# Due times of the output projections in an attention and feed-forward block

## The chip, the core and the metric

The kernel runs on one core of a Trainium2 chip. The time is the device time of one execution in microseconds (us), and the figure quoted is the median of several executions. Five engines run side by side, each through its own instructions in a fixed order: TensorE (PE in the profile; its weight loads are listed as PEld), VectorE (DVE), ScalarE (ACT), GpSimd (POOL) and SyncE (SP), which here only issues transfers. An instruction waits until what it depends on is done, and everything behind it on its engine waits too.

## The reference

The input is x of 4 batches, 1024 rows and 512 columns, in 32-bit floats. There are two halves, each wrapped in layer norms and added back to its input:

```python
x = x + layernorm(attn(layernorm(x)))
x = x + layernorm(ffn(layernorm(x)))

def attn(x):                       # 16 heads of 32
    q, k, v = split(x @ Wqkv + bqkv)
    scores = einsum("bsnh,btnh->bnst", k, q) / sqrt(32)
    scores = triu(scores) + -10000.0 * tril(ones, k=-1)
    attn = softmax(scores, axis=2)
    out = einsum("bnkq,bknh->bqnh", attn, v)
    return out @ Wo + bo
```

The feed-forward half multiplies by gate and up weights of 2048 x 512 and a down weight of 512 x 2048, held as small integers with a zero point and scales. The change touches the attention half only.

## The kernel before

**Periods.** The four batches are worked off one after another. In each, four groups of four heads (the index `hb`, also called a head block here) follow each other. A head block takes 12 *periods*: 4 for the first 512 rows of the softmax axis (`g` is 0) and 8 for the second (`g` is 1). So there are 48 periods a batch and 192 in all, numbered `p` from 0; 12 more (-12 to -1) lead in. In this text the *phase* of a period is `p` modulo 12. In one period the program issues, in this order:

- `weights` for one tile of 128 keys, in two halves `u` of two heads each: PE puts minus the maximum (L359) and the scores (L367) into PSUM, ACT takes the exponential (L384), and in the periods on the diagonal (phases 0 to 3 and 8 to 11) POOL cuts off the triangle (L386);
- `maxima` for a tile that is 12 periods ahead: PE scores (L278), on the diagonal a bound on DVE (L286), and the reduction on DVE (L290);
- `values` of the period before: exponentials times v (PE L406), added up in `po`;
- `add_up`: the exponentials of the tiles are summed for the softmax denominator, by an accumulating transfer issued from POOL (L434) off the diagonal and by POOL additions (L436) on it;
- at the end of phases 3 and 11, `shift_parts`: a chain of small DVE instructions (L300 to L306) that turns the maxima into what the next tiles' exponentials subtract.

Pieces of other work are put in between, by a small planner.

**The planner.** Work with a cost and a due period stands in three queues called lanes: `qk` and `v` (a piece is one projection of 128 columns by 256 rows for four heads, 64 matmuls at L250 in 16 groups of 4, evacuated by ACT at L532 or L535) and `out` (a piece is `project_out(b, j, half)`). Each piece costs `FULL`, 1.75. Every period a budget `spare` grows by `rate(p)`, which is the steepest slope of cost to be done over time left; `fill` takes the lane whose first piece is due earliest as long as the budget allows, or when the piece is already due. A lane is first in, first out. `fill(p, 1)` can put one piece in the middle of a period (after the `weights`, `maxima` and `values` of `u` 0), and `fill(p, 9)` puts the rest at its end. In what follows a piece in the middle is marked @0 and a piece at the end @2. Apart from these, at most one of the `whole` pieces goes into a period: a stage of the layer norm (`ln_stage`; from the fourth on it has four PE transposes, L515), the transposes of v (`turn_piece`, L544), the scan of v on DVE (`later_v`, L552), the transposes of the maxima (`shift_rows`, L314) and the part of the masked keys (`masked_part`, L326). A `turn_piece` can go only once the v pieces it needs are out, and a scan only once its turns are.

**An output projection.** `project_out(b, j, half)` computes half the columns of 128 rows of batch b. Its instructions: for half 0 a load of the input rows `xo` on SP (256 KB, L560); on PE 64 matmuls at L250 into `py`; on DVE the bias addition that empties `py` into `y` (L567); and for half 1 the following. First `store_out(b, j - 1)` for the rows before: DVE normalizes `y` (L86), POOL adds `y` to `xo` (L579), SP stores `xo` (L580, 256 KB). Then the statistics of its own `y`: DVE L76 and L77, POOL L79 and L80. `y` and `xo` have two buffers each, so the first L567 of rows j + 1 needs the L579 of rows j - 1 done. `y`'s PSUM tile comes from `projected`: the first piece of a half period uses a bank of its own (`ps_own`), and any further one the two buffers of `ps_big`, which it shares with the `maxima` tiles, with the second `weights` tile of some periods and with the transposes.

**Where they stand.** `after` is the first period of the next batch, `at[b, 0, 0] + 48`. The pieces of batch b may start at `after - 3` (rows 0 to 511, j under 4) or `after + 5` (j from 4 on). All 16 are due at `after + 39`:

```python
due = after + 39
put(lanes["out"], FULL, min(due, n_periods - 1 if j < 4 else n_periods + 9),
    lambda p, t=after - 4 + WAIT if j < 4 else after + 4 + WAIT: p >= t,
    project_out, b, j, half)
```

In the order that comes out, the pieces of batch 0 stand in periods 59 (one), 70 and 71 (three) and 78 to 85 (twelve); those of batch 1 in 107, 118, 119 and 126 to 133; those of batch 2 in 171 to 183, one or two in each; those of batch 3 in 189 to 191 and after the last period. Below, a piece is written OUT b j half: OUT 0 4 1 is `project_out(0, 4, 1)`.

## Time and profile before

| | |
|---|---|
| median of 3 runs | 1933.15 us (1932.91 to 1935.1) |
| time of the profiled execution | 1933.34 us |
| its span, first to last instruction | 1931.6 us |
| mean granted TensorE clock | 0.989 |
| periods 0 to 191 begin at | 79.2 to 1186.2 us |
| DVE busy, whole span | 1223.6 us (63%) |
| ACT busy | 643.1 us (33%) |
| POOL busy | 715.4 us (37%) |
| DVE busy from 344.6 to 635.1 us (batch 1) | 222.4 of 290.5 us |
| POOL busy in the same stretch | 162.2 of 290.5 us |

A period is found in the trace by L359: 768 matmuls, four in each period, so the start of every fourth one begins a period. In the lines of the profile, a group of instructions is named by line, engine and operation, and `out<-in` gives the program's names; in a timeline the first two numbers are start and duration in us, and a bracket gives how long the engine had been idle and what released it.

### The profile page before, as it was taken

The numbers are of one execution on the slowest core, as the hardware profiler recorded it, in microseconds if no ns is written. First come the engines' busy times: TensorE is split into PE (matmuls) and PEld (weight loads), VectorE is DVE, ScalarE is ACT, GpSimd is POOL, SyncE is SP. The second block draws the span as 40 slices with busy tenths as digits, with TensorE's granted clock in tenths as the row PEclk, the third lists the DMA queues.
The fourth block names the chain that finished last, engine by engine and source line by source line (L and its number), as shares of the span: only waits on it lengthen the run. The fifth ranks groups of instructions, "written<-read, shape, count | busy, mean of one in ns | idle before, by whom it ended". The sixth has DMA issues, their size and how long they took to land.

```text
span 1931.6 us, 40959 instructions
## 1 busy us (share of the span) xinstructions
PE 1851.4 (96%) x17761; PEld 1095.2 (57%) x17761; DVE 1223.6 (63%) x1913; ACT 643.1 (33%) x962; POOL 715.4 (37%) x1016
## 2 busy tenths in 40 slices
PE   7899999999989999989999989999999999999997
PEld 3334444444444444444344434788888888888886
DVE  4788888887777777777777875544344444444344
ACT  2244444434424444424444322222222222222221
POOL 2155545554655564655455474102010110101011
PEclk9899999999999999999999999999999999999999
DMA  3254355345245145245134452511010100101000
GB/s 110 66 127 104 79 127 121 79 115 99 49 112 115 25 87 100 59 102 100 23 67 89 116 135 71 190 66 44 1 44 4 41 12 33 40 5 44 1 22 24
DMA packets 65628, 137.48 MB, mean 71 GB/s; under 512 B 6304, under 2 KB 20640, under 8 KB 65440
## 3 DMA queue, kind: packets, MB, share of 16 engines
q0 software_dynamic: 17280, 62.92, 17.6%
q1 hardware_dynamic: 41008, 67.40, 10.5%
q10 hardware_dynamic: 7152, 4.46, 0.8%
q8 instruction: 141, 2.31, 0.5%
q14 instruction: 47, 0.39, 0.1%
HBM read 55.07 MB, written 16.78 MB: 37 GB/s over the span
## 4 chain that ended last, share of the span: by engine, by line
PE 83%; DVE 7%; POOL 5%; ACT 2%; issue 2%; DMA 2%; POOLq 0%; SPq 0%; DVEq 0%
PE pq L250 17%; PE pg L973 12%; PE pu L973 12%; PE acc L1006 12%; PE sc L278 9%; PE po L406 6%; PE st L359 4%; PE st L367 3%; PE py L250 2%; PE pd L417 2%; DVE nm L290 2%; POOL pT L436 1%; ACT pT L384 1%; DMA pT<-pT 1%; POOL xo L579 1%
## 5 line engine op out<-in xcount | busy, mean ns | idle before, releaser
L384 ACT ACTIVATE pT<-st 128x1024 f32<-128x1024 f32 (+3 forms) x384 | 310.2, 811 | 367.7 <-PE st L367 286.8
L290 DVE TENSOR_REDUCE nm<-sc 128x2 f32<-128x1024 f32 (+3 forms) x384 | 366.7, 956 | 102.4 <-PE st L367 82.6
L250 PE MATMUL pq<-xnT,w 128*32 128x256 f32 x6144 | 377.8, 391 | 3.5 <-ACT xnT L516 2.7
L278 PE MATMUL sc<-in,in 32*128 32x512 f32 (+3 forms) x1536 | 346.5, 537 | 16.4 <-DVE nm L290 13.3
L367 PE MATMUL st<-in,in 32*128 32x512 f32 (+3 forms) x1536 | 306.2, 487 | 0.0
L250 PEld LDWEIGHTS pq<-xnT,w 128*32 128x32 f32 x6144 | 186.5, 112 | 204.7 <-issue 83.8
L983 DVE SCALAR_TENSOR_TENSOR h<-pu,pre_us,s 128x512 f32<-128x512 f32 x128 | 96.1, 751 | 311.0 <-PE pu L973 310.2
L1006 PE MATMUL acc<-d,h 128*128 128x512 f32 x896 | 224.8, 393 | 0.2 <-DVE h L993 0.2
L386 POOL TENSOR_SCALAR_AFFINE_SELECT pT<-pT 128x256 f32<-128x256 f32 x256 | 131.8, 538 | 248.9 <-ACT pT L384 248.8
L981 ACT ACTIVATE s<-pg,pre_gs 128x512 f32<-128x512 f32 x128 | 88.1, 688 | 297.7 <-PE pg L973 297.7
L1006 PEld LDWEIGHTS acc<-d,h 128*128 128x128 f32 x896 | 166.0, 188 | 34.2 <-DVE h L993 0.5
L436 POOL TENSOR_TENSOR pT<-pT,pT 128x768 f32<-128x768 f32 (+1 forms) x120 | 183.5, 1550 | 1.8 <-DMA pT<-pT 1.8
L286 DVE TENSOR_TENSOR sc<-sc,bound 128x256 f32<-128x256 f32 x256 | 109.1, 426 | 118.2 <-PE sc L278 76.4
L406 PE MATMUL po<-pT,vt 128*32 128x512 f32 (+3 forms) x1536 | 170.6, 496 | 12.0 <-POOL pT L386 9.6
L79 POOL TENSOR_SCALAR rs_y<-mv_y 128x1 f32<-128x1 f32 x32 | 8.7, 271 | 448.1 <-DVE mv_y L77 448.1
L434 POOL DMA_DIRECT2D pT<-pT x120 | 106.5, 916 | 152.2 <-PE pm L314 57.4
L992 ACT CAST h<-h 128x512 fp32r<-128x512 f32 x128 | 79.4, 621 | 248.4 <-DVE h L983 248.4
L993 DVE TENSOR_TENSOR h<-h,h 128x512 fp32r<-128x512 f32 x128 | 88.7, 693 | 87.9 <-ACT h L992 87.9
L359 PE MATMUL st<-mT,ones_bf 3*128 3x512 bf16 (+3 forms) x768 | 125.4, 331 | 13.8 <-ACT pT L384 13.8
L278 PEld LDWEIGHTS sc<-in,in 32*128 32x128 f32 x1536 | 114.5, 185 | 35.8 <-issue 12.4
L367 PEld LDWEIGHTS st<-in,in 32*128 32x128 f32 x1536 | 134.0, 190 | 0.7
L250 PE MATMUL py<-wo_sb,o 128*32 128x256 f32 x2048 | 121.5, 384 | 7.1 <-DVE y L567 5.1
(136 smaller groups left out, 2572.2 us busy)
## 6 DMA issues: line engine op xcount, KB each, us to landing
pT<-pT POOLq DMA_DIRECT2D x120, 512.0 KB, 5.7
xr<-in_x SPq DMA_DIRECT2D x32, 256.0 KB, 2.8
xo<-in_x SPq DMA_DIRECT2D x32, 256.0 KB, 2.9
x<-xo SPq DMA_DIRECT2D x32, 256.0 KB, 2.0
out<-y SPq DMA_DIRECT2D x32, 256.0 KB, 2.0
look<-in_gate_wt SPq DMA_DIRECT2D x16, 256.0 KB, 3.1
look<-in_up_wt SPq DMA_DIRECT2D x16, 256.0 KB, 2.7
look<-in_down_wt SPq DMA_DIRECT2D x16, 256.0 KB, 3.0
```

Of the source, the lines that this page charges most:

```text
L250: nc.tensor.matmul(out[k * D : (k + 1) * D, :], lhsT=lhsT[:, k * D : (k + 1) * D], rhs=rhs, start=(c == 0), stop=(c == len(pairs) - 1),)
L278: nc.tensor.matmul(sc[:, h % 2, :n], lhsT=qT[h * D : (h + 1) * D, ts(j, P)], rhs=kT[h * D : (h + 1) * D, 512 * k : 512 * k + n], start=Tru ...
L286: nc.vector.tensor_tensor(sc[:, :, n - P : n], sc[:, :, n - P : n], bound.unsqueeze(1).to_broadcast((P, 2, P)), ALU.min,)
L290: nc.vector.tensor_reduce(nm[:, k, jj, 2 * u : 2 * u + 2], sc[:, :, :n], AX.X, ALU.max, negate=True)
L359: nc.tensor.matmul(st[h // 2][:, h % 2, :n], lhsT=ones_bf[h * D : h * D + 3, :], rhs=mT[h * D : h * D + 3, 512 - n :], start=True, stop=False,
L367: nc.tensor.matmul(st[h // 2][:, h % 2, :n], lhsT=kT[h * D : (h + 1) * D, ts(c, P)], rhs=qT[h * D : (h + 1) * D, q0 : q0 + n], start=False ...
L384: nc.scalar.activation(pT[:, :, :n], st[u][:, :, :n], AF.Exp)
L386: nc.gpsimd.affine_select(out=pT[:, :, :P], in_=pT[:, :, :P], compare_op=ALU.is_ge, fill=0.0, base=0, pattern=[[0, 2], [1, P]], channel_mu ...
L406: nc.tensor.matmul(state["po"][h * D : (h + 1) * D, 512 - n :], lhsT=v[:, c, h * D : (h + 1) * D], rhs=pT[:, h, :n], start=(c == 0), stop= ...
L436: nc.gpsimd.tensor_tensor(total[:, :, 512 - n :], total[:, :, 512 - n :], pT[:, :, :n], ALU.add)
L973: nc.tensor.matmul(dst, lhsT=w[i * P // IB][:, c, ts(i % (IB // P), P)], rhs=part[:, c, :], start=(c == 0 and k == 0), stop=(c == HC - 1 a ...
L1006: nc.tensor.matmul(acc[t0][t], lhsT=part[:, ts(t, P)], rhs=dw[i * P // IB][:, i % (IB // P), :], start=(i == 0 and k == 0), stop=(i == IC ...
```

## The change

One line: the pieces of a batch are no longer all due at `after + 39` but one every second period, from `after + 7` to `after + 37`.

```diff
             for j in range(NJ):
                 for half in range(2):
-                    due = after + 39
+                    due = after + 7 + 4 * j + 2 * half
                     put(lanes["out"], FULL, min(due, n_periods - 1 if j < 4 else n_periods + 9),
                         lambda p, t=after - 4 + WAIT if j < 4 else after + 4 + WAIT: p >= t,
                         project_out, b, j, half)
             put(lanes["out"], 0.1, due + 1,
                 lambda p, b=b: state.get(("rows at", b, NJ - 1), p) < p, store_out, b, NJ - 1)
```

Nothing else is edited. The number of instructions on each engine stays as it was; the planner puts them in another order from period 50 on. For the last batch the due times are cut to 191 and 201 as before. The pieces of batch 0 now stand in periods 50 to 84, of batch 1 in 97 to 132, of batch 2 in 146 to 178, and the pieces of q, k and v, the stages of the layer norm and the turns of v move to other periods in between. Periods 176 and 179 to 184 hold none of these pieces any more, where before 176 to 183 held ten output projections.

## The prediction

> **What bounds the kernel now.** The page comes first: PE is busy nearly all the time and fills the chain that ended last. Then the waits of PE and DVE in the attention part, from 344 to 1186 us.

> ```profile
> span 1931.6 us, 40959 instructions
> ...
> PE 1851.4 (96%) x17761; PEld 1095.2 (57%) x17761; DVE 1223.6 (63%) x1913; ACT 643.1 (33%) x962; POOL 715.4 (37%) x1016
> ...
> PE 83%; DVE 7%; POOL 5%; ACT 2%; issue 2%; DMA 2%; POOLq 0%; SPq 0%; DVEq 0%
> ```

> ```profile
> PE py L250 <- DVE y L567: 4.8, 4, 1.4
> PE sc L278 <- DVE nm L290: 3.9, 4, 1.9
> PE sc L278 <- DVE y L567: 3.1, 2, 1.5
> PE pv L544 <- DVE y L567: 2.6, 2, 1.4
> ```

> The reader sees that moving PE work as such gains nothing, and that part of PE's few waits (4.8 + 3.1 + 2.6 = 10.5 us) comes from DVE's emptying of `py`.

> Next I cut the trace into periods by the starts of L359. Their lengths repeat to a hundredth: phase 7 with one piece and one transposing piece takes 5.81 us twelve times, with a second piece 7.53 to 7.54; phase 8 takes 5.47, with transposes 6.18. So a length is a floor of its phase, plus 1.73 a piece, plus 0.66 to 0.7 for transposes, plus a *stall*. The counts of pieces and transposes don't change; only stalls do. Over periods 48 to 179 I add up 41.8 us of them. A quiet phase 0 beside one in the burst of output projections (us from the start, length, busy times, clock):

> ```profile
> core 0: us, PE busy (x) PEld busy (x) DVE busy (x) ACT busy (x) POOL busy (x), PEclk, DMA share, GB/s
> 562.58:572.19 9.61, 6.88 (x97) 3.14 (x94) 8.72 (x20) 2.05 (x2) 5.40 (x8) 1.00 0.15 56
> 635.12:640.54 5.42, 4.88 (x66) 2.16 (x64) 5.14 (x10) 2.05 (x2) 4.59 (x7) 1.00 0.01 3
> ...
> 441.40:445.10 3.70, 3.70 (x34) 1.39 (x34) 2.83 (x5) 0.00 (x0) 1.42 (x3) 0.54 0.24 44
> ```

> The first has one piece more (1.73) and still 2.46 us too many, with DVE at 8.72 of 9.61: on the diagonal DVE is the second bound. The last row is a stretch in which the clock was halved; I come back to it. What stalls in the burst (timeline):

> ```profile
> 553.04 3.79 POOL L436 TENSOR_TENSOR pT<-pT,pT 128x768 f32<-128x768 f32 x2
> ...
> 554.23 0.93 DVE L86 TENSOR_SCALAR y<-y,mv_o 128x512 f32<-128x512 f32 x1
> ...
> 556.80 1.26 POOL L579 TENSOR_TENSOR xo<-xo,y 128x512 f32<-128x512 f32 x1
> ...
> 558.09 0.42 DVE L567 TENSOR_TENSOR y<-py,bo_sb 128x256 f32<-128x256 f32 x1 [2.12 <-POOL xo L579]
> 558.57 0.30 PEld L278 LDWEIGHTS sc<-in,in 32*128 32x128 f32 x4 [1.73 <-DVE y L567]
> ```

> `y` has two buffers. The piece OUT j 1 normalizes and stores rows j - 1; the piece OUT j+1 0 needs that buffer. POOL adds `xo` only after two denominator sums; DVE waits 2.12 us at L567, its maxima behind it wait, and PE's scores behind those. I call OUT j 1 and OUT j+1 0 in one period a *pair*. The last view is the small chain on DVE after phases 3 and 11:

> ```profile
> 945.47 2.50 POOL L436 TENSOR_TENSOR pT<-pT,pT 128x512 f32<-128x512 f32 x2
> 945.60 1.19 DVE L304 TENSOR_TENSOR nm<-nm,wide 128x16 f32<-128x16 f32 x1
> 946.82 1.21 DVE L305 CAST wide<-nm 128x16 bf16<-128x16 f32 x1
> ...
> 949.62 0.30 PEld L278 LDWEIGHTS sc<-in,in 32*128 32x128 f32 x4 [2.70 <-DVE nm L290]
> ```

> Beside POOL's sums these take 1.2 us each; at 564.49 and 564.71, without them, 0.18 and 0.20. PE's scores wait.

> [...]

> **The change, part by part** (positions from the order of instructions of both kernels and the planner's loop).

> *Taken away.* The bursts in periods 80 to 85 and 128 to 132 had stalls of 6.94 and 6.96 us. The turn in period 148 (4.65, the last view) moves to 151, phase 7, where turns stalled 0.00. Periods 172 to 174 had 2.05 with output pieces of batch 2 in them. Sum -20.6.

> *The tail.* Periods 180 to 184 took 25.5 us with five pieces; less 5 x 1.73 that is 16.9. They lose all five. Their floors add up to 16.15; without the maxima (four score matmuls of about 1 us together, four periods) and with three transposes, some 14. So up to -2.9; no wait takes over as long as ACT (2.05 in a phase 0) is under PE. If the cover of the pieces was hiding an exponential's delay, 0. I take -2.0.

> *Turns pushed to the head block's end.* The q, k and v pieces go later, so the turns of the third batch's and second batch's last head block land in phases 11 and 0 (83 and 84, 131 and 132), the scan in phase 2 and the masked part in phase 3 (87, 135). Periods 35 to 41 have just this order, and stall 4.64 us. Twice: +9.3. If the second pieces beside them cover it, 0.

> *Pairs in phases 0 and 4, in the middle and at the end of the period.* Periods 72, 76, 120 and 124. Nearest row: period 84 (OUT 0 6 1 and OUT 0 7 0), 2.46, with 0.51 in the next. Bound below: period 119, two pieces without this wait in it, 0 and 0.25 in the next; above: 131's 3.70. With 2.97 each: 11.9, less the 2.46 that these four places stall today (72: 0.84; 76: 0.67; 120 and 121: 1.47; 124: -0.52): +9.4.

> *Pairs at the end of phase 8.* Periods 80, 128 and 164. Nearest: the pairs at the end of phase 9 (81, 129), after which 82 and 130 stalled 1.38 and 1.20: +1.3 each, +3.9. Bounds 0 and 2.06 (period 83).

> *A turn in period 100, phase 4,* behind a short phase 3. Turns and transposes in phase 4 stalled -0.1 (52), 0.67 (76), 2.96 (112) and 4.65 (148). Where no long phase 3 goes before it is 3 or more: +3.0.

> *Single half-1 pieces where DVE is tight.* In 63, 111, 155, 159 and 167 a piece brings DVE 0.42 (L567) + 0.59 (L86) + 0.69 (L76) + 0.18 (L77) = 1.88 us. All of it on the path would be 9.4, none 0 (phase 7's pieces, 79 and 127, stalled 0.00); half: +4.7.

> *At nothing.* ACT is idle 3.5 us at a time, so its moved evacuations wait on PE alone. On SP each `xo` load stands behind the store of the rows two before, and the loads of the layer norm and of the weight check queue behind it; they are due a period (4 to 9 us) later and land in 2.8 to 3.1, so a late one would first show as DVE waiting at L76 or L589, up to 3 us. On POOL, L579, L79 and L80 (1.3 + 0.3 + 0.6) go ahead of L434's transfers in phases 5 to 9; three `pT` buffers cover that.

> Sum: -20.6 - 2.0 + 9.3 + 9.4 + 3.9 + 3.0 + 4.7 = +7.7 us, on a span of 1931.6. The profiled execution took 1933.34, the median is 1933.15, so the times differ by nothing that matters: 1940.9.

> *The clock.* In periods 64, 112, 131 and 148 the granted clock was halved for 3.4 us, each time after PE's weight loads had paused 1.73 to 2.70 us; 32 matmuls at L250 took 3.56 instead of 1.93, so it costs 1.7. Some sixteen pauses over 1.5 us gave four of these. Seven new pauses would give 1.7 x 7 / 4 = 3.0, but two of the four lie in what is taken away and are in its sum; I leave the new ones to the range.

> [...]

> **The rivals.**

> - *Faster.* The wait for `y` needs POOL to be behind with two sums. In phases 0 and 4 the piece in the middle of a period stands ahead of that period's sums, so L579 may come at once. With 0.25 a pair, and none in phase 8: 7.7 - 4 x 2.72 - 3.9 = -7.1, 1926. It decides once a pair costs under 2.97 - 7.7 / 4 = 1.05 us. Against it: in period 84, the same place, L567 still waited for DVE's own chain.
> - *No change.* One kind of stall for another, as the 13.9 and 12.1 us of stalls in batches 1 and 2 suggest, however their pieces lie: 1933, give or take 3.
> - *Slower still.* Every one of the seven pairs' pauses halves the clock: 7 x 1.7 = 11.9 more, 1952.8. Against it: four in sixteen so far.
> - That it doesn't do what it says is out: the order of instructions shows the pieces spread.

> **How the numbers follow.** Forecast 50 in 100, no change 24, faster 18, slower still 8. The time is the forecast's. A measurement of this kernel tells apart about 0.2%, 3.9 us. Faster by more: 0.19; within: 0.24; slower by more: 0.57. The range leaves out the last case and half of the faster one: 1926 to 1949.

> **What would show it.** In the changed kernel, no DVE wait at L567 in periods 81 to 85; waits at L567 for POOL L579 in 72, 76, 120, 124 and after 80, 128, 164; PE waiting at L326 in 87 and 135; period 100 near 9 us and 148 at 5.4; 180 to 184 at about 15 us together. I am wrong if the pairs pass without a pause, or if other phases' floors move, which would mean that the sum by phases doesn't hold.

## The result, and the profile after

| | before | after |
|---|---|---|
| median | 1934.12 us (4 runs, 1932.91 to 1936.32) | 1959.16 us (4 runs, 1958.22 to 1963.16) |
| ratio | | 1.0132, 95% interval 1.0115 to 1.015 |
| span of the profiled execution | 1931.6 us | 1957.6 us |
| mean granted clock in it | 0.989 | 0.981 |
| half clock within periods 0 to 191 | 17.1 us, 5 windows | 54.6 us, 16 windows |

The kernel became 25 us slower; the forecast was 7.7 us. First the page of the kernel after, the lines that were shown of before:

```profile
span 1957.6 us, 40968 instructions
...
PE 1868.5 (95%) x17761; PEld 1102.3 (56%) x17761; DVE 1222.8 (62%) x1913; ACT 642.8 (33%) x962; POOL 710.3 (36%) x1016
...
PE 83%; DVE 10%; POOL 4%; issue 1%; ACT 1%; DMA 1%; SPq 0%; POOLq 0%; DVEq 0%; ACTq 0%
```

The number of matmuls is the same, yet PE is busy 17 us longer: the same matmuls took longer, as in the windows of half clock, where 32 of L250 take 3.41 us (at 495.25, shown below) instead of the 1.93 of full clock (at 1117.38 of before). DVE's share of the chain rose from 7 to 10%. Then the waits of the attention part, 344 to 1212 us (what waits <- for what: total us, times, longest):

```profile
PEld py L250 <- DVE y L567: 13.8, 5, 3.4
...
PE po L406 <- POOL pT L386: 9.8, 9, 3.1
PE py L250 <- DVE y L567: 9.6, 4, 2.6
...
PE sc L278 <- DVE nm L290: 6.6, 6, 2.5
PEld pd L417 <- DVE y L567: 6.1, 4, 2.6
```

PE's wait of L250 for L567 has doubled (4.8 to 9.6 us), and the row sums of the softmax (`pd`, L417) wait for L567 too. Three stretches of the kernel after: period 72, a pair; period 84, which was in the burst and took 9.61 us; and period 177 in the tail, which took 7.43 us before.

```profile
core 0: us, PE busy (x) PEld busy (x) DVE busy (x) ACT busy (x) POOL busy (x), PEclk, DMA share, GB/s
...
488.38:498.59 10.21, 8.08 (x96) 3.50 (x93) 9.33 (x17) 2.05 (x2) 6.63 (x10) 0.83 0.07 25
568.37:576.69 8.32, 8.32 (x100) 3.97 (x97) 6.97 (x13) 2.52 (x3) 1.87 (x4) 1.00 0.01 2
...
1139.60:1154.11 14.51, 9.65 (x61) 2.77 (x61) 7.53 (x10) 1.62 (x2) 10.59 (x16) 0.65 0.98 217
```

Periods 72 and 177 of the kernel before, for comparison (84 of before was shown with the prediction):

```profile
484.90:491.16 6.26, 4.98 (x64) 2.07 (x60) 5.95 (x15) 2.05 (x2) 5.93 (x9) 1.00 0.46 128
1111.83:1119.25 7.42, 6.19 (x64) 2.28 (x61) 7.05 (x11) 1.62 (x2) 7.34 (x10) 1.00 1.02 242
```

In period 84 PE is now busy throughout: the burst is gone, as forecast. The other two stall, at a granted clock of 0.83 and 0.65. In period 177 POOL is busy 10.59 of 14.51 us.

The period model (floor + 1.73 a piece + transposes + stall) held: in both kernels periods without a stall agree to some 0.05 us. So the 26 us of span can be put down place by place, as the change of the stalls from before to after (windows of half clock that fall there in brackets, before and after). The second profile of after, from the fifth experiment, stands beside it.

| periods | forecast | after | second profile |
|---|---|---|---|
| bursts and turn: 80-85, 128-132, 148, 172-174 | -18.0 (-20.6, and +2.6 for the pairs in 80 and 128) | -17.4 (2; 0) | -17.5 |
| pairs in phases 0 and 4: 72, 76, 120, 124 and the next | +9.4 | +9.7 (0; 3) | +9.5 (3) |
| turns at the block's end: 86-91, 133-139 | +9.3 | +4.3 (0; 1) | +4.3 (1) |
| turn in 100 | +3.0 | +3.2 (0; 1) | +1.6 (0) |
| single pieces: 60-69, 105-119, 145, 155-171 | +4.7, and 1.3 for 164 | +18.7 (2; 4) | +18.5 (4) |
| tail, 175-184 | -2.0 | +9.0 (0; 5) | +9.6 (6) |

The rows of the first profile add up to +27.5 us. All periods together grew by 28.0, and the stretch ahead of period 0, where no output piece stands, was 2.7 us shorter in it (76.49 us instead of 79.15). Four terms came near or stayed below; the single pieces and the tail are what was missed, 13 and 11 us. The timeline of the pair in period 72:

```profile
489.85 1.21 DVE L304 TENSOR_TENSOR nm<-nm,wide 128x16 f32<-128x16 f32 x1
...
490.05 1.90 PE L250 MATMUL py<-wo_sb,o 128*32 128x256 f32 x30
491.09 1.22 DVE L305 CAST wide<-nm 128x16 bf16<-128x16 f32 x1
...
493.04 1.23 DVE L290 TENSOR_REDUCE nm<-sc 128x2 f32<-128x1024 f32 x1
...
494.78 0.41 DVE L567 TENSOR_TENSOR y<-py,bo_sb 128x256 f32<-128x256 f32 x1
...
495.25 3.41 PE L250 MATMUL py<-wo_sb,o 128*32 128x256 f32 x32 [2.13 <-DVE y L567]
```

The first piece is through PE at 491.95, but DVE empties it only at 494.78, behind the small chain and the maxima. The second piece stands first in its half period, so it takes the same bank, `ps_own`, and PE waits. Then it runs at half clock: 32 matmuls take 3.41 us where 30 took 1.90. That isn't the wait of the forecast, which had DVE wait at L567 for a buffer `y` that POOL still read. Between 344 and 1212 us that wait came up 1.1 us in all, in periods 81 and 165. And the tail, period 177:

```profile
1142.61 1.06 POOL L386 TENSOR_SCALAR_AFFINE_SELECT pT<-pT 128x256 f32<-128x256 f32 x1
...
1143.00 3.07 POOL L485 TENSOR_TENSOR o<-t,t 128x128 f32<-128x128 f32 x1
1143.43 2.85 POOL L79 TENSOR_SCALAR rs_f<-mv_f 128x1 f32<-128x1 f32 x1
1143.56 2.28 DVE L552 TENSOR_TENSOR_SCAN vl<-in,zero 128x1024 f32<-128x1024 f32 x1
...
1143.73 1.92 PE L406 MATMUL po<-pT,vt 128*32 128x512 f32 x4 [3.15 <-POOL pT L386]
...
1146.91 0.40 POOL L386 TENSOR_SCALAR_AFFINE_SELECT pT<-pT 128x256 f32<-128x256 f32 x1
```

PE waits for the triangle cut L386, which stands on POOL behind a store's L579, L79 and L80, and again behind an L485 and an L79 that take 3.07 and 2.85 us here, beside a DVE scan of 2.28 (the median of the 124 L485 is 0.46). With no output piece in 176 PE gets there early, its weight loads pause 3.76 and 3.45 us, and it then runs at half clock. In the kernel before, where two pieces stand in 176, the same two waits of PE's matmuls were 0.62 and 0.61 us, against 3.15 and 1.71 here:

```profile
1113.83 1.05 PE L406 MATMUL po<-pT,vt 128*32 128x512 f32 x4 [0.62 <-POOL pT L386]
...
1115.49 1.05 PE L406 MATMUL po<-pT,vt 128*32 128x512 f32 x4 [0.61 <-POOL pT L386]
```

The pieces that the forecast took out of the tail had been work under which POOL caught up.

### The profile page after: what moved, and what is told of

It reads as the page before. It is cut to its first block, busy times and chain, and to the rows that moved or that the text cites. A ratio compares the mean times of both kernels' runs of the same rounds, so it can differ in the third digit from the quotient of the medians.

```text
span 1957.6 us, 40968 instructions
## 1 busy us (share of the span) xinstructions
PE 1868.5 (95%) x17761; PEld 1102.3 (56%) x17761; DVE 1222.8 (62%) x1913; ACT 642.8 (33%) x962; POOL 710.3 (36%) x1016
## 3 DMA queue, kind: packets, MB, share of 16 engines
q0 software_dynamic: 17280, 62.92, 17.4%
## 4 chain that ended last, share of the span: by engine, by line
PE 83%; DVE 10%; POOL 4%; issue 1%; ACT 1%; DMA 1%; SPq 0%; POOLq 0%; DVEq 0%; ACTq 0%
PE pq L250 16%; PE pg L973 12%; PE pu L973 12%; PE acc L1006 12%; PE sc L278 9%; PE po L406 6%; PE py L250 4%; PE st L359 4%; PE st L367 3%; DVE nm L290 2%; PE pd L417 2%; DVE sc L286 1%; POOL pT L436 1%; ACT pT L384 1%; PE pv L544 1%
## 5 line engine op out<-in xcount | busy, mean ns | idle before, releaser
L290 DVE TENSOR_REDUCE nm<-sc 128x2 f32<-128x1024 f32 (+3 forms) x384 | 366.7, 956 | 102.5 <-PE st L367 83.3
L250 PE MATMUL pq<-xnT,w 128*32 128x256 f32 x6144 | 377.1, 390 | 4.0 <-ACT xnT L516 2.7
L278 PE MATMUL sc<-in,in 32*128 32x512 f32 (+3 forms) x1536 | 348.7, 541 | 15.7 <-DVE nm L290 15.7
L250 PEld LDWEIGHTS pq<-xnT,w 128*32 128x32 f32 x6144 | 187.1, 112 | 199.1 <-issue 78.6
L386 POOL TENSOR_SCALAR_AFFINE_SELECT pT<-pT 128x256 f32<-128x256 f32 x256 | 125.9, 508 | 259.4 <-ACT pT L384 259.3
L436 POOL TENSOR_TENSOR pT<-pT,pT 128x768 f32<-128x768 f32 (+1 forms) x120 | 183.5, 1550 | 0.2 <-DMA pT<-pT 0.2
L79 POOL TENSOR_SCALAR rs_y<-mv_y 128x1 f32<-128x1 f32 x32 | 8.7, 270 | 448.2 <-DVE mv_y L77 448.2
L434 POOL DMA_DIRECT2D pT<-pT x120 | 106.4, 925 | 157.0 <-PE pm L314 60.8
L250 PE MATMUL py<-wo_sb,o 128*32 128x256 f32 x2048 | 129.3, 399 | 12.0 <-DVE y L567 9.9
L359 PE MATMUL st<-mT,ones_bf 3*128 3x512 bf16 (+3 forms) x768 | 126.7, 334 | 10.6 <-ACT pT L384 10.0
L278 PEld LDWEIGHTS sc<-in,in 32*128 32x128 f32 x1536 | 115.2, 186 | 36.7 <-issue 15.9
```

Source lines behind the costliest of these rows:

```text
L250: nc.tensor.matmul(out[k * D : (k + 1) * D, :], lhsT=lhsT[:, k * D : (k + 1) * D], rhs=rhs, start=(c == 0), stop=(c == len(pairs) - 1),)
L278: nc.tensor.matmul(sc[:, h % 2, :n], lhsT=qT[h * D : (h + 1) * D, ts(j, P)], rhs=kT[h * D : (h + 1) * D, 512 * k : 512 * k + n], start=Tru ...
L290: nc.vector.tensor_reduce(nm[:, k, jj, 2 * u : 2 * u + 2], sc[:, :, :n], AX.X, ALU.max, negate=True)
L359: nc.tensor.matmul(st[h // 2][:, h % 2, :n], lhsT=ones_bf[h * D : h * D + 3, :], rhs=mT[h * D : h * D + 3, 512 - n :], start=True, stop=False,
L386: nc.gpsimd.affine_select(out=pT[:, :, :P], in_=pT[:, :, :P], compare_op=ALU.is_ge, fill=0.0, base=0, pattern=[[0, 2], [1, P]], channel_mu ...
L436: nc.gpsimd.tensor_tensor(total[:, :, 512 - n :], total[:, :, 512 - n :], pT[:, :, :n], ALU.add)
```

## The experiments

Ratios are against before, run on the same chips, with 95% intervals. Experiments 1 to 4 ran together (before 1935.26 us, 17 runs), 5 to 8 together (1934.03, 8 runs), 9 to 11 together (1936.18, 14 runs). Experiments 5, 6 and 9 are one run each and are read by their profiles. "Stalls" of some periods are their time over the floors of the period model.

### 1. ScalarE empties the output pieces

```diff
-            nc.vector.tensor_tensor(y[:, ts(half, 256)], py, bo_sb[:, ts(half, 256)], ALU.add)
+            nc.scalar.copy(y[:, ts(half, 256)], py)
+            nc.vector.tensor_tensor(
+                y[:, ts(half, 256)], y[:, ts(half, 256)], bo_sb[:, ts(half, 256)], ALU.add
+            )
```

> The changed kernel, but ACT copies each output projection out of PSUM into y (a copy of 128x256, about 0.47 us as the q, k, v pieces take there), and DVE then adds the bias in place in SBUF. Theory 1 (the bank): the projection stays in its one PSUM bank until DVE, busy with the chain L300 to L306, comes to L567, and PE's next piece or the denominator sums L417 wait for that bank. Then the pauses in periods 72, 76, 120, 124, 157, 161 and 169 go, with their half clocks: 1940 to 1946 us, and PE's waits for DVE's L567 (13 us from 344 us on) under 3 us. Theory 2 (the buffer y, the prediction's): y is not free until POOL has added xo; ACT then waits just as DVE did, with the exponentials behind it: 1957 to 1965 us, pauses in the same periods.

Measured: 1962.77 us (1957.06 to 1963.74), 1.0131 [1.0111, 1.0151]: no gain. The four pairs fell from 12.2 to 4.2 us and 157, 161 and 169 from 7.9 to 2.7, as the bank theory has it. But 60 to 69 and 105 to 119 grew by 3.1 and 6.1, and ACT waited for the buffer, PE behind it (waits of this kernel, same stretch). Of the 6.1 us, 4.2 stand in period 105, and 105 grew by 4.2 and 3.7 in experiments 6 and 9 too, where DVE empties as in after: that part can't be put down to the edit.

```profile
ACT y L567 <- POOL xo L582: 16.6, 6, 3.3
...
PEld pd L417 <- ACT y L567: 10.3, 5, 2.6
```

So there are two obstacles in a row: the bank that DVE empties late, and behind it the buffer `y` of the forecast. Freeing the first brings the second to light.

### 2 and 3. Only batches 0 and 1, or only batch 2

```diff
-                    due = after + 7 + 4 * j + 2 * half
+                    due = after + 7 + 4 * j + 2 * half if b < 2 else after + 39
```

(and `b == 2` in the third)

> The new due times for batches 0 and 1 alone; batch 2 is due as before. By the stalls added up period by period, batches 0 and 1 cost 16 us of the 26: 1950 us, give or take 3, with periods 176 to 181 as in the kernel before (8.3 us of stalls). If the loss lies in the emptied tail alone: 1934 to 1938.

> The new due times for batch 2 alone. By the stalls: 10 to 12 us, 1945, give or take 3, of which 9 in periods 176 to 181. If the emptied tail costs nothing and its stalls are those of the layer norm stages, as the prediction had it: 1932 to 1937.

Measured: 1951.36 us (1948.52 to 1955.0), 1.0088 [1.0068, 1.0108], and 1941.25 us (1937.07 to 1944.41), 1.0031 [1.0021, 1.0041]. The first came as expected, the second lay just under its range. The two add up to 1.0119, near the whole change's 1.0132. With batch 2 alone, the tail still went from 5.9 to 13.7 us of stalls, with four windows of half clock: the tail's loss comes from batch 2's pieces leaving it. Its size depends on the profile of before, in which no half clock fell in the tail: in experiments 2, 4 and 8, where the tail's pieces stand as in before, 175 to 184 took 4.3, 4.3 and 2.5 us longer than there, with two, two and one windows. Beside these the tail's loss in after is 5 to 7 us, not 9.

### 4. One piece a period in chosen places

```diff
-                    due = after + 39
+                    due = after + (2, 5, 6, 7, 8, 9, 17, 18, 19, 20, 21, 29, 30, 31, 32, 33)[2 * j + half] if b < 2 else after + 39
+                    t = after - 4 + WAIT if j < 4 else after + 4 + WAIT
...
-                        lambda p, t=after - 4 + WAIT if j < 4 else after + 4 + WAIT: p >= t,
+                        lambda p, t=due if b < 2 else t: p >= t,
...
-                ahead = heads(lanes, p)
+                ahead = heads({k: w for k, w in lanes.items() if k != "out" or most != 1 or p > 144}, p)
```

(against before; the last edit keeps output pieces out of the middle of a period)

> Batches 0 and 1: one piece in each of the periods after + 2, 5 to 9, 17 to 21 and 29 to 33 (phases 5 to 9, and one phase 2), always at the end of the period; batch 2 due as before. Theory 1: in these phases no denominator sum waits for the bank and DVE has no chain, so the bursts' 13.9 us go and only the turns moved to phases 11 and 0 come back (2 to 5 us a batch): 1926, from 1921 to 1931. Rival (spreading costs wherever the pieces stand, because every period then loses cover of another kind): 1940 or more.

Measured: 1940.76 us (1938.46 to 1944.45), 1.0028 [1.0017, 1.0038]: theory 1 missed, the rival's time (1940 or more) came. Bursts (13.9 to 5.5 us) and pairs were gone, but new stalls came in 57 to 59 (6.3 us), 87 (2.3), 105 and 106 (4.3) and 135 (3.8): a second half in phases 7 to 9 puts L579, L79 and L80 (2.1 us on POOL) ahead of the scan and the triangle.

### 5. The kernel after, a second profile

> The kernel after, unchanged, profiled a second time. Theory C (most of what the forecast missed is the granted clock: a pause of PE does or does not bring a window of half clock of about 3.4 us, by where the pause falls on a grid of windows that runs freely): the pauses of PE's weight loads are the same as in the first profile to 0.1 us wherever no half clock lies just before them, but the half clock falls in other periods in part, each window shifts the length of its period by about 1.55 us, and the span differs from 1957.6 us by up to 6 us. Rival (what is slow is fixed by the order of the work): the same periods with the same lengths to 0.1 us, half clock included.

Measured: 1957.82 us, span 1956.1. Periods 36, 100 and 120, first in the first profile of after, then in the second (the columns as above):

```profile
270.53:279.61 9.08, 8.38 (x69) 3.47 (x66) 7.77 (x11) 2.52 (x3) 2.95 (x4) 0.82 0.01 2
...
660.28:669.61 9.33, 8.33 (x69) 3.14 (x66) 7.71 (x11) 2.52 (x3) 6.04 (x9) 0.82 0.00 0
789.34:798.22 8.88, 6.51 (x97) 3.42 (x94) 8.54 (x17) 2.05 (x2) 5.51 (x8) 1.00 0.01 2
```

```profile
272.98:280.52 7.54, 6.84 (x68) 2.93 (x66) 7.25 (x11) 2.52 (x3) 2.95 (x4) 1.00 0.01 2
...
659.23:666.91 7.68, 6.69 (x68) 2.76 (x65) 7.54 (x11) 2.52 (x3) 6.03 (x9) 1.00 0.00 0
788.34:798.44 10.10, 7.76 (x96) 3.38 (x93) 9.30 (x17) 2.05 (x2) 6.37 (x10) 0.83 0.07 26
```

The same instructions, 1.54 and 1.65 us shorter without half clock, and 1.22 longer with it (0.7 net, as the next period gave 0.5 back). The total of half clock after period 48 is the same, 47.8 us, in other places. That agrees with theory C: a pause is where a window of half clock *may* follow, and the program's order alone does not decide whether it does.

### 6 and 9. Filling the pairs' pauses with useless work

> After, with 64 useless matmuls of 1.9 us in all into an unused half of the PSUM bank, just ahead of the second output piece of periods 72, 76, 120 and 124, where PE paused 2.95 to 3.41 us. Theory C: what remains of each pause is 1.0 to 1.5 us, no half clock follows it there, and the four periods are not longer than in after although PE has 1.9 us more to do in each: 8.5 to 8.8 us each. Rival (a pause costs its own length only, the half clock in these periods came from something else): half clock as before in them, and periods longer by up to 1.9 us each. Theory B (the bank is what the second piece waits for): its wait ends at the same time after the first piece as in after, filled or not.

Measured: 2016.32 us. As an experiment on the pauses it failed. A piece is 16 matmul calls (32 in the trace's records, 2048 for 64 pieces), not the 64 that this text gave above; the 64 stood in an order in which none overlaps, took 14 us a time, and waited for L567 like the piece behind them. So once more:

```diff
+            if p in (72, 76, 120, 124):
+                t = ps_big.tile([P, 256], F32, tag="big", name=f"fill_{p}")
+                for c in range(HC):
+                    for k in range(P // D):
+                        nc.tensor.matmul(
+                            t[k * D : (k + 1) * D, :],
+                            lhsT=wo_sb[:, c, k * D : (k + 1) * D],
+                            rhs=wo_sb[:, c, 256:512], start=True, stop=True,
+                        )
             fill(p, 9)
```

> The filler of the sixth experiment was of the wrong size and in the wrong place: 64 matmuls in an order in which they don't overlap, 14.3 us of PE a time, and into the bank under dispute, so that they waited for VectorE too (22.5 us in all). Here after, with the 16 matmuls of one projection piece more (1.73 us by the period model), useless, into another bank, just ahead of the second output piece of periods 72, 76, 120 and 124. Theory C: PE's pauses there shrink from 2.95 to 3.41 us to 1.2 to 1.7 us, and with them the half clock: at most one of the four periods has a window of it, where the two profiles of after have one in or behind three of the four; and no period is longer than its own period in after that had a half clock, though each has 1.73 us more work: 72, 76, 120, 124 and the period behind each cost 10.8 us over their floors and the filler's 6.9 together, against 12.2 and 10.9 in after without any filler. The filler's own time is then covered: the sum over these eight periods is longer than in after by less than 3 us. Rival (the pauses cost their length, the clock is not of their making): longer by 5 to 7 us, half clock as before.

Measured: span 1956.4 us (time 1958.13). Period 72 and 76 with the filler, then 76 without it, in the first profile of after (72 was shown above):

```profile
488.00:497.62 9.62, 8.33 (x128) 4.50 (x125) 9.28 (x17) 2.05 (x2) 6.41 (x10) 1.00 0.02 7
513.45:522.41 8.96, 8.11 (x128) 3.88 (x124) 8.75 (x16) 2.05 (x2) 5.28 (x8) 1.00 0.01 2
```

```profile
514.30:524.21 9.91, 7.35 (x96) 3.20 (x93) 9.19 (x16) 2.05 (x2) 6.15 (x10) 0.90 0.03 10
```

32 matmul records more, and both periods are shorter, at full clock. The eight periods (72, 76, 120, 124 and the next of each) took 63.7 us together, against 66.2 and 66.0 in the two profiles of after, though PE had 6.9 us more to do; half clock there fell from 10.2 us to none. Theory C expected up to 3 us more; they came out 2.4 us less. The whole was not faster than after: half clock fell elsewhere, and 105 and 112 grew by 3.7 and 1.1 us.

### 7. No output pieces in phases 0 and 4

```diff
-                        lambda p, t=after - 4 + WAIT if j < 4 else after + 4 + WAIT: p >= t,
+                        lambda p, b=b, t=after - 4 + WAIT if j < 4 else after + 4 + WAIT: (
+                            p >= t and (b == B - 1 or p % 12 not in (0, 4))
+                        ),
```

> After, with the output pieces of the first three batches barred from phases 0 and 4 of a batch (they go when the next phase opens). Theory B (in these phases the second piece, and the row sums of the softmax behind it, take the one PSUM bank that the first half of the period left full): the pauses of PE in 72, 76, 120, 124, 157, 161 and 169, 12 us together over before in the four pairs and 6 in the three others, go, and little comes in their place, since the pieces go into phases that had none: 1943 us, 1938 to 1948. Rival M (a piece costs the same wait wherever it stands, as in the experiment that gave the emptying to ScalarE): 1955 to 1962 us.

Measured: 1945.18 us (1941.57 to 1949.63), 1.0062 [1.0039, 1.0085], as theory B expected. The pairs' 12.2 us went to -0.6, and 157, 161 and 169 from 7.9 to 1.0; 87 and 135 stalled 5.1 and 3.9 us, with half clock (4.1 and 1.3 in after), and the tail kept its stalls (14.4 in 175 to 184, 14.9 in after). Where a piece stands was worth 14 us of the 25.

### 8 and 11. Two more placements

> One output piece a period, of batches 0 and 1, at the periods 2, 5, 6, 7, 17, 18, 19, 29 to 34, 37, 38 and 39 after the batch's softmax is done, none in phases 0 and 4 and none as a burst; batch 2 as before. It leaves the turns of batch 1 nearly where they were before. Theory B: bursts, bank waits and late turns are all gone, and what is left is half clock at pauses shared with before: 1930 us, 1924 to 1936, below before. Rival M: a piece in the first half of a period delays the POOL or DVE work of that phase by its own 2.1 us wherever it stands, as it did in periods 57 to 59, 87 and 105 of the run with single slots: 1938 to 1946 us.

Measured: 1942.25 us (1938.04 to 1944.3), 1.0043 [1.0028, 1.0058], in the rival's range. The pieces were moved to 2, 5, 6, 7, 17, 18, 19, 29 to 34, 37, 38 and 39 in the diff of experiment 4. PE now waited 3.6 us for the scan in 58 and in 106, each time with half clock behind it.

> Output pieces of batches 0 and 1 at 18, 22, 23, 26, 27, 29, 30, 34, 34, 35, 35, 37, 37, 38, 38 and 39 periods after the batch's softmax is done (batch 2 as before): none in phases 0 and 4, no second half of a tile in phases 7 to 9 where its store on POOL would stand ahead of the scan and the diagonal, and late enough that the q, k and v pieces, the turns and the masked part of the next batch stand where they did in before up to its burst. Theory B: the stalls by the output pieces are then those of pairs in one half period, 0.1 to 0.5 us each, 14 us of burst fall to 4, and half clock at pauses that before has too stays: 1924 us, 1918 to 1930. Rival M (pairs at the end of a half period stall like a burst wherever they stand): 1931 to 1940 us.

Measured: 1939.82 us (1936.62 to 1942.37), 1.0017 [1.0007, 1.0027]. The time is in rival M's range, but both theories miss a part. The bursts of 13.9 us fell to 9.9 only: PE's scores wait for L567 behind pairs at the end of the period before (84: 4.3 us and 87: 3.7, each with half clock; 131 and 135: 2.0 each). And batch 2 did not stay quite as before: one piece moved from 176 to 177, and 177 took 13.97 us with waits of 2.92 and 3.48 us for L386, the tail's loss again (+4.3 us over 175 to 184). Three placements by hand ended 4 to 8 us behind the one in which the pieces pile up at the end.

### 10. The kernel before, emptied by ScalarE

The first experiment's diff, on before.

> The kernel before, with ScalarE emptying the projection's bank (a copy) and VectorE adding the bias in place. In before PE's waits for VectorE's emptying of an output piece are some 12 us, nearly all in the two bursts (periods 80 to 85 and 128 to 132, 13.9 us over their floors). Theory Q (these waits are VectorE's queue, and ScalarE has room there): the bursts cost 4 to 8 us less: 1927 us, 1923 to 1931. Rival (as in the first experiment with after: the wait is as much for the buffer y, which POOL's store still reads, and a ScalarE that waits for y holds up its exponentials): no gain, 1933 to 1941 us.

Measured: 1945.24 us (1941.23 to 1946.13), 1.0047 [1.0032, 1.0062]; slower still than the rival. The bursts did not shrink (13.9 to 15.6 us, three windows of half clock for one), and 178 and 181 grew by 3.6 each. Of these, 178 grew as much in experiments 2 and 4, where nothing is changed there, and bursts left as in before stalled 15.5 and 15.8 us in experiments 3 and 12. So the 9 us between the medians are clear of the spread, but where they arise stays open. Moving a wait to another engine did not pay in either kernel.

### 12. The kernel before, with its pauses filled

```diff
+        def warm(p):
+            t = ps_own.tile([P, 256], F32, tag="own", name=f"warm_{p}")
+            by_columns(t, [(wo_sb[:, c], wo_sb[:, c, 256:512]) for c in range(HC)])
...
+                if u and p in (36, 64, 112, 148):
+                    warm(p)
                 if unit and now:
                     maxima(*unit, [1 - u])
...
+                        if p in (4, 178):
+                            warm(p)
                         values(*before)
```

> The kernel before, with the 16 useless matmuls of one projection piece (1.73 us, into the idle bank of the projections) at six places where PE of before pauses 1.5 to 2.7 us with nothing to do: ahead of the scores of the second half of periods 36, 64, 112 and 148 and ahead of the value products of periods 4 and 178. Nothing else is changed. Theory C: the pauses there are filled, and with them goes the half clock, which the profile of before has in four of these six periods and other profiles of the same code in the two others, 1.55 us a window: 1929 us, 1925 to 1932, below before. Rival (the filler costs what it takes wherever a pause is shorter than it, and half clock comes by other pauses instead): 1933 to 1939 us.

Measured: 1929.10 us (12 runs, 1925.62 to 1932.28) against 1935.19 (17 runs): 0.9971 [0.9961, 0.9981]. Periods 64 and 112, first in before, then with the filler:

```profile
436.01:445.10 9.09, 8.00 (x68) 3.18 (x66) 8.09 (x13) 3.01 (x4) 4.48 (x7) 0.81 0.10 18
725.90:734.95 9.05, 7.96 (x70) 3.26 (x67) 8.09 (x13) 3.01 (x4) 4.49 (x7) 0.82 0.10 26
```

```profile
431.00:439.34 8.34, 8.15 (x100) 3.67 (x97) 8.08 (x13) 3.01 (x4) 4.47 (x7) 1.00 0.01 3
720.00:728.34 8.34, 8.16 (x101) 3.67 (x98) 8.07 (x13) 3.02 (x4) 4.46 (x7) 1.00 0.05 6
```

0.7 us shorter with 1.73 us more work, at full clock. 4 and 148 fell likewise, by 1.6 each. 36, which had no half clock before, grew by 1.1; 178, where PE's weight loads still paused 3.22 us behind the filler, got half clock now (+2.5). This version beats both kernels, by useless work. That rests on the medians: in the two profiles periods 0 to 191 took the same time to 0.2 us, since windows also fell elsewhere (128 to 132 grew by 2.0), and 4.4 of the 4.6 us between the spans lie ahead of period 0, where no filler stands.

### 13. The kernel after, with its pauses filled

A helper like that of experiment 12, with the bank and the number of pieces chosen by place, called once in 4, 36, 72, 76, 112, 120, 124, 157, 161 and 169, twice in 64 and four times in 177.

> The kernel after, with useless matmuls of whole projection pieces (16 of them, about 1.73 us each, 27.7 us of PE in all) where PE pauses: one piece each in periods 4, 36, 72, 76, 112, 120, 124, 157, 161 and 169, two in 64, and four in 177 (two ahead of each of its two waits of 3.8 and 3.5 us for POOL). Nothing else is changed, so POOL's and DVE's delays are all still there. Theory C (half clock is a large part of what the change costs): some eleven windows of half clock go, at 0.95 to 1.55 us each, less 2 to 4 us where a filler is longer than its pause: 1949 us, 1944 to 1953, faster than after although PE has 27.7 us more to do; period 177 takes 10 to 12 us where it took 14.5. Rival S (the pauses themselves are nearly all of it, half clock hardly matters since PE waits anyway): 1958 to 1970 us, 177 unchanged.

Measured: 1956.59 us (4 runs, 1951.57 to 1960.35), 1.0116 [1.009, 1.0141], beside a before of 1936.54 (7 runs). The median missed both. It is 2.6 us below that of after (1959.16), and the two intervals overlap (after: 1.0115 to 1.015), so a gain over after is not shown by the times. The profiled execution is the fastest of the four (span 1949.9 us). In it half clock after period 48 fell from 47.8 to 10.2 us. Period 177 there:

```profile
1134.32:1146.37 12.05, 12.05 (x188) 6.25 (x188) 7.43 (x10) 1.62 (x2) 9.18 (x13) 1.00 0.95 219
```

Four useless pieces more, and 12.05 us instead of 14.51. But before took 7.43: of the 7.1 us that 177 lost, at least 2.5 were the clock's and at most 4.6 are POOL's delay itself. Over this one profile, the fastest, the fillers gave some 8 us back, net of what they cost where they outlast the pause (1.3 and 1.4 in 157 and 169).

### How the 25 us divide

Every execution comes with its mean granted clock. Over 130 executions of twelve kernels, compared within each kernel, 0.001 of clock is worth 1.14 us (correlation -0.77); of the 61 of before, those at 0.986 have a median of 1937.0 us, those at 0.990 of 1932.9. One window of 3.41 us at half clock takes 0.0009 off the mean, so it costs about 1.0 us on average, less than the 1.54 and 1.65 by which periods 36 and 100 differed in experiment 5. Before has a median clock of 0.988, after of 0.981: 7 x 1.14 = 8 us. The filled profile of experiment 13 gives some 8 as well, but the median of its four runs only 2.6, at a median clock of 0.989; both are net of what the fillers cost where they outlast a pause. So about 3 to 8 of the 25 us are half clock, and the larger part are the waits that bring it. The 8 is an average over kernels, and a finer division stays open.

## Why the prediction was wrong, step by step

- *The bursts and the turn in 148*: right. -20.6 and the two pairs beside them made -18.0; -17.4 came. L567 waits for L579 there once, in 81, for 0.6 us at most, and 148 takes 5.42.
- *The tail*: the step that failed outright. "no wait takes over as long as ACT (2.05 in a phase 0) is under PE" looked at ACT alone; the wait that took over was PE's for POOL (L386, 3.76 and 3.45 us in 177), which the term put at nothing. The term -2.0 measured +9.0 and +9.6, or 5 to 7 beside tails of before with half clock. The loss began in 177, ahead of the stretch that was costed (180 to 184 took 19.4 us, not 15). Experiment 3 shows that batch 2's pieces do it, experiment 11 that moving one piece from 176 to 177 is enough, experiment 13 that at most 4.6 of 177's 7.1 us are the delay and the rest the clock.
- *Turns at the block's end*: over-sized, +4.3 for +9.3. PE did wait at L326 in 87 (2.02 us, with half clock behind it), but not in 135 (0.1 us). In the row taken as the pattern, periods 35 to 41, 36 and 41 stall 1.5 and 1.3 us; their counterparts 84 and 132 stalled 0.5 and 1.1, and 89 and 137 nothing.
- *Pairs in phases 0 and 4*: right in size (+9.7 for +9.4), by a wrong cause. It was the bank, emptied late by DVE, not `y` and POOL. The size fits because the row that it was taken from already had the bank's wait in it: in period 84 of before PE's weight loads stood 1.60 and 2.23 us at L250 for L567, and L567 itself only 0.58 us for L579. That three windows of half clock are in the +9.7 is luck too. Experiment 1 shows that `y` stands just behind it, and experiment 7 that the place is what matters.
- *Pairs at the end of phase 8*: 0.3, 0.3 and 0.4 us instead of 1.3 each. The second piece of an end-of-period pair takes another bank.
- *The turn in 100*: +3.2, of which 1.65 was half clock (the second profile has 1.6).
- *Single pieces*: mis-sized by 13 us, a term of +4.7 (and 1.3 for 164) that measured +18.7 and +18.5 with what stood around it. Half of DVE's 1.88 us was charged, in five periods, as if nothing else waited. The stalls came one period later and elsewhere: 64, 105, 108, 112, 157, 161, 169. Period 64 is the mechanism of the forecast: L567, L86, L76 and L77 of a single piece stand on DVE ahead of the maxima, and PE's scores wait 3.29 us for L290 instead of 1.74, now with two windows of half clock instead of one. In 105 PE waits for POOL's L386, in 108 for L567; how much of these and of 112 the single pieces make stays open. In 157, 161 and 169 the row sums take the very bank that the single piece had filled (in 157 the trace puts the wait down to L386, but that had ended 0.9 us earlier, and PE starts as L567 ends); that experiment 7 removes.
- *The clock, left to the range*: the second mis-size. It was costed at 3.0 for seven new pauses and then left out of the sum; about 3 to 8 us came. The quarter of the pauses was read off pauses of 1.5 us and more; the new ones are 2 to 3.8 us long. In the profile of after, between 344 and 1212 us, PE's weight loads paused that long 12 times from full clock, and half clock came behind 9 of them.

The rival "slower still" came closest in time (1952.8), and for half of its reason: half clock behind the new pauses, though not the pairs' alone. Faster failed on the pairs, "no change" on single pieces and tail.

## What to carry to other kernels

When work that fills gaps is moved, cost the gap it leaves: which engine was catching up under it (here POOL), and how long the bottleneck will now pause. A pause of TensorE can have a second price at the clock: half clock came behind 9 of the 12 pauses of its weight loads of 2 to 3.8 us in after, and behind 1 of 3 of 2.2 to 2.7 in before. A pause that can't be removed can be filled with useless matmuls of its own length, into a bank that nothing waits for (worth 0.3% in experiment 12, nothing clear of the spread in 13). Ask of every added piece which single-buffered tile it takes and who takes it next.

## What the hardware showed that was not expected

| PE busy in the window | windows | followed by half clock |
|---|---|---|
| over 80% | 2625 | 0 |
| 60 to 80% | 181 | 20 |
| 40 to 60% | 56 | 32 |
| under 40% | 23 | 23 |

Before and after alone have 439, 28, 11 and 4 such windows, and 0, 4, 5 and 4 of them were followed by half clock. So by these counts what matters is how much of one window a pause takes: a pause of about 2 us that lies in one window leaves PE busy for some 40% of it at most, while two windows that share it evenly keep some 70% each. That would explain why the same code has half clock in one execution and not in the next. Where the longest pause of PE within a window was 1.6 to 1.8 us, half clock followed 10 of 17 times; in before and after alone it was 1 of 3 times, and 6 of 6 where the pause was longer.
